# First layer of a two-layer graph network: SyncE's loads tied to steps of their own turn, half the buffers for a chunk's node rows, and a reordered turn

## The chip, the cores and the metric

The kernel runs on one core of a Trainium2 chip. The time of a run is that of the device, from the start of the program to its end, in microseconds (us). Lower is better. The kernel before was run three times; beside these there is one execution taken by the hardware profiler, and all durations below are from that one.

The engines that matter are PE (TensorE, matrix products), DVE (VectorE), ACT (ScalarE), POOL (GpSimd, which does nothing in this kernel's loops but issue indirect DMAs that gather rows) and SP (SyncE, which issues all other DMAs). Each engine works through its own list of instructions in order. A wait on a semaphore holds up everything behind it on that engine.

## What is computed

There are 12,500 nodes with 128 features, and 400,000 edges sorted by the node at which they end (`dst`). Two layers follow one another; the change concerns the first, an edge and node perceptron, with a sum over the edges of each node:

```python
h = jnp.maximum(_layernorm(x, axis=-1), 0.0)
# _L0_gnn_ref
src_f = node_features[src]
dst_f = node_features[dst]
edge_in = jnp.concatenate([src_f, dst_f, edge_features], axis=1)
h = jax.nn.relu(edge_in @ We1 + be1)
edge_msg = jax.nn.relu(h @ We2 + be2)
node_in = jnp.concatenate([dst_f, edge_msg], axis=1)
h2 = jax.nn.relu(node_in @ Wn1 + bn1)
node_msg = jax.nn.relu(h2 @ Wn2 + bn2)
agg = jax.ops.segment_sum(node_msg, dst, num_segments=node_features.shape[0])
return node_features + agg
```

The second layer normalises the nodes again, multiplies each by eight matrices (one for each type of edge), gathers for every edge the row of its source and type, weighs it and sums by `dst`:

```python
H = jnp.einsum('ni,rio->rno', h, W)
msg = (H[etype, src] + b[etype]) * norm
out = jax.ops.segment_sum(msg, dst, num_segments=h.shape[0])
```

The eight products of a node are made in the first layer already, as soon as its sum is complete, and written to a table in HBM (`tab_h`).

## The kernel before

**Stages.** Up to about 130 us the nodes are normalised and multiplied, and two tables are written: `tab_a`, a row of 32 numbers per node for its part as a source in the first product, and `tab_cb`, a row of 96 for its part as an end in the first and third products. Then the first layer runs up to about 5433 us, and the second from there to the end. The second layer is bound by its own gathers on POOL (line 1019) and is the same in both kernels.

**Tiles.** Edges are taken in chunks of 1024 (8 tiles of 128), 391 in all. Three chunks make a span (131 spans). The edges of a span end in a window of nodes; a window's sums stand in one PSUM tile, `acc`, while the span's chunks are added to it. A window's end rows are read from `tab_cb` as a [126, 96] tile of bfloat16, 23.6 KB per chunk, `win`.

**The work of a chunk** is a class, `Edges`, whose methods are steps:

- `load_win` (L402): SP loads `win`, from a ring of 8 buffers.
- `ends_T` (L406): DVE compares the chunk's ends with the window's rows and writes a 0/1 matrix `ohT`.
- `gather_a` (L387): POOL issues eight indirect DMAs, each for 128 sources' rows of `tab_a`, into `gb`, a ring of 16. POOL can so run up to 16 chunks ahead of the rest.
- `first` (L420, L422): PE multiplies the edge features by their weights into the PSUM bank `pre` and adds the ends' part, `win` times `ohT`.
- `first_src` (L427, L431): DVE transposes `gb` to `agT`, which frees the gather's buffer, and adds it to `pre`, giving `z`. `first_end` (L435): ACT makes `h1` from `z`.
- `second` (L442, L447): PE products into banks `pm0` and `pm1`, and ACT to `em`.
- `third` (L453, L456, L459): PE products `win` x `ohT` and `em` x weights into bank `u`, and ACT to `h2`. This is the last step that reads `win`.
- `fourth` (L466): PE products into `pq0` and `pq1`. `fourth_sum` (L474, L475): DVE adds the bias, ACT takes the positive part rounded to PE's short form. `fourth_end` (L480): DVE takes what the rounding left out.
- `ends` (L485): DVE writes a 0/1 matrix `oh`. `fifth` (L494): PE adds the chunk to `acc`.

**The work of a span.** `head(s)` (L588) loads a span's five addresses from SBUF to SP's registers. `load_relb` (L595) brings 756 KB, repeated over partitions, which `ends_T` reads. `load_eat` (L602) brings 768 KB of edge features, which `first` reads. Both have two buffers. `Span(s)` (L687) loads the 128 nodes of the window, 64 KB, `xt`; `deviate` and `begin` normalise them. When the span's `acc` is complete, `end` sums it, and `rows_h` (L546 to L567) goes on as a generator, a piece at each `node_step()`: deviation, normalisation, a PE transpose into a bank (L558), ACT to `hT`, two PE products of 512 columns (L565), and SP's write of the rows to `tab_h` (L567), 576 KB.

**PSUM** has eight banks with one buffer for each name: `pre`, `pm0`, `pm1`, `u`, `pq0`, `pq1`, `acc`, and one with constants. A step that writes a bank waits for those who read it last.

**The loop** (L746 to L779) runs in turns. In turn i the chunk i is gathered and has its first product; chunk i-1 has its second and third, chunk i-2 its fourth and its values, and chunk i-3 is added up. With `s, k = divmod(i, 3)`, a turn has k = 0, 1 or 2. After the loop a written-out tail finishes the last chunks. At its end one call fixes the order on SP, DVE, ACT and PE to that of the program:

```python
in_order(start, ENG.SP, ENG.DVE, ENG.Activation, ENG.PE)
```

So the order of calls in a turn is the order on each queue. POOL's own order is that of the program too. `next(prepared)` hands out small pieces of a preparation for the second layer, one per turn in the earlier part of the loop.

Of the kernel before, what the change touches and what calls it, by code (L numbers as in the profile page):

```python
# [8 lines left out]
F32 = mybir.dt.float32  # L9
F32R = mybir.dt.float32r  # L10
BF16 = mybir.dt.bfloat16
# [9 lines left out]
P = 128  # L21
# [32 lines left out]
def gnn_kernel(  # L54
# [337 lines left out]
    class Edges:  # L392
# [5 lines left out]
            self.pool, self.psum, self.iota, self.node = pool, psum, iota, node  # L398

        def load_win(self, row):  # L400
            self.win = self.pool.tile([WR, 96], BF16, name="win", bufs=8)
            nc.sync.dma_start(in_bytes(self.win), row)  # L402

        def ends_T(self, relb):
# [165 lines left out]
    with tc.tile_pool(name="e0", bufs=2) as pool, \  # L570
# [5 lines left out]
        nc.vector.tensor_copy(nid_p, nid)  # L576
        chunks, spans, rows, relbs, eats = {}, {}, {}, {}, {}
        active = []
        before = [None]

        def node_step():
# [3 lines left out]
        def head(s):  # L585

            if s < NS:
                _, rows[s] = nc.values_load_multi_w_load_instructions(  # L588
                    heads[0:1, s, :], engines=[ENG.SP], min_val=0, max_val=RX * ROW * (N - 1),
                    skip_runtime_bounds_check_because="a least dst is a node")  # L590
# [89 lines left out]
        class Span:  # L680


            def __init__(self, s):
                _, _, _, at_x, at_h = rows.pop(s)
                self.to = from_byte(tab_h, at_h, P, N - 1)
                self.xt = pool.tile([P, D], F32, name="xt")
                nc.sync.dma_start(in_bytes(self.xt), from_byte(x, at_x, P, N - 1))  # L687

            def deviate(self):
# [5 lines left out]
            def end(self, left):  # L695

                before[0] = summed(pool, self.acc, "a20")
                banks = ("u", "u", "u") if left else ("pre", "pm0", "pm1")
                steps = rows_h(pool, psum, self.to, self.x0, before[0], banks)
                active.append(steps)  # L700
                if left:
                    node_step()
                else:
                    next(steps)
                    next(steps)
# [25 lines left out]
        def end_T(c):  # L731
            chunks[c].ends_T(relbs[c // SC][:, c % SC, :])
# [1 line left out]
        def first(c):  # L734
            chunks[c].first(eats[c // SC][:, c % SC, :])

        head(0)
        load_relb(0)
        load_eat(0)
        for c in range(AHEAD):  # L740
            load(c)
        end_T(0)


        L = NC - 1
        for i in range(L):  # L746
            s, k = divmod(i, SC)
            if k == 0:
                head(s + 1)
                load_relb(s + 1)  # L750
            load(i + AHEAD)
            if k == 1:
                load_eat(s + 1)
                spans[s] = Span(s)
            gb = gathered(i)
            first(i)
            if i > 0:
                chunks[i - 1].second()
            whole = sum_up(i - 3) if i > 2 else None
            chunks[i].first_src(gb)  # L760
            if i > 1:
                chunks[i - 2].fourth()
            if i > 0:
                chunks[i - 1].third()
            chunks[i].first_end()
            end_T(i + 1)
            if i > 1:
                ends(i - 2)
            if i % SC == 0:
                node_step()  # L770
            if i > 1:
                valued(i - 2)
            if i % SC == 0 and i:
                spans[i // SC - 1].deviate()
            node_step()
            if whole:
                whole.end(NC - (i - 2))
            if i % SC == 1 and i > 1:
                spans[i // SC - 1].begin()  # L779
            next(prepared, None)  # L780


# [4 lines left out]
                if L - c:  # L787
                    spans[c // SC + 1].begin()

        for s in range((L - 1) // SC, NS):  # L790
            if s not in spans:
                spans[s] = Span(s)
            spans[s].deviate()
        spans[(L - 1) // SC].begin()
        gb = gathered(L)
        first(L)
# [313 lines left out]
```

## Time and profile before

| | us |
|---|---|
| median of 3 runs | 9815.11 (9800.64 to 9815.46) |
| profiled execution | 9814.24 |
| its span in the profile | 9812.5 |
| PE busy | 3925.3 (40%) |
| DVE busy | 5313.4 (54%) |
| ACT busy | 1657.7 (17%) |
| POOL busy | 6275.8 (64%) |
| first layer's gathers on POOL, last start | 5265.75 |
| second layer's first gather | 5433.08 |

The profiled execution lies within 1 us of the median. A busy share is an average over both layers; the two have different limits. For the first layer, the following view gives each engine's busy time in two stretches, one while POOL still gathers and one after its last gather (length, busy us of PE, PEld, DVE, ACT and POOL, each with its number of instructions, PE's granted clock, the DMA engines' share, GB/s):

```profile
5100.00:5200.00 100.00, 61.50 (x230) 28.77 (x226) 55.03 (x99) 26.74 (x51) 58.15 (x62) 0.79 0.27 80
5300.00:5340.00 40.00, 35.59 (x151) 16.05 (x150) 34.95 (x61) 17.04 (x31) 0.00 (x0) 1.00 0.17 58
```

In the first stretch no engine is busy for more than 62% of the time; in the second PE and DVE are busy for close to 90%.

In a row of the costliest groups, the figures are busy time and mean duration (ns), then the idle time of that engine just before these instructions, and what ended most of it. "<-remote" means that a semaphore ended the wait that the profile can't put down to an instruction of this core's engines. In timelines, brackets hold the same for one instruction.

### The profile page before, as it was taken

How to read it: one execution, taken by the hardware profiler on the slowest of the kernel's cores; microseconds unless marked ns; L12 is line 12 of the kernel's file. 1: busy time of each engine (PE TensorE's matmuls, PEld its weight loads, DVE VectorE, ACT ScalarE, POOL GpSimd, SP SyncE). 2: the span in 40 equal slices, each digit the busy share in tenths (PEclk: the TensorE clock that was granted, in tenths of full speed). 3: DMA queues.
4: the chain of work that ended last, by engine and by line, in shares of the span. 5: the costliest groups of instructions: out<-in, count | busy, mean ns of one | idle time of the engine just before them, and what ended most of it. 6: DMA issues, size and time to landing. Idle time of an engine off the chain costs nothing.

```text
span 9812.5 us, 56126 instructions
## 1 busy us (share of the span) xinstructions
PE 3925.3 (40%) x13981; PEld 1895.2 (19%) x13982; DVE 5313.4 (54%) x8291; ACT 1657.7 (17%) x3217; POOL 6275.8 (64%) x6273
## 2 busy tenths in 40 slices
PE   2566666666666666666667100000000000000000
PEld 1233333333333333333233000000000000000000
DVE  4455555555555555555557555555555555555554
ACT  2222222222222222222223000000000000000000
POOL 6555555555555555555552677777777777777776
PEclk6777777777777777777778555555555555555555
DMA  3233332222222222222222111111111111111111
GB/s 120 74 87 66 72 72 72 70 65 68 66 66 66 71 71 66 67 66 69 64 72 77 56 51 51 51 51 51 51 51 51 51 51 51 51 51 51 51 51 46
DMA packets 605555, 614.49 MB, mean 63 GB/s; under 512 B 361633, under 2 KB 465893, under 8 KB 604767
## 3 DMA queue, kind: packets, MB, share of 16 engines
q1 hardware_dynamic: 403064, 353.77, 11.8%
q0 software_dynamic: 200192, 256.65, 10.4%
q8 instruction: 114, 1.87, 0.1%
q14 instruction: 221, 1.80, 0.1%
q10 hardware_dynamic: 1964, 0.41, 0.0%
HBM read 509.91 MB, written 100.43 MB: 62 GB/s over the span
## 4 chain that ended last, share of the span: by engine, by line
POOL 32%; PE 20%; another core or an unknown queue 17%; issue 17%; DVE 8%; ACT 4%; DMA 2%; DVEq 0%; POOLq 0%; SPq 0%; ACTq 0%
POOL hg L1019 31%; PE pq L466 5%; PE acc L494 3%; PE pm L442 3%; PE pre L420 3%; DVE nm L480 2%; ACT em L447 2%; PE u L456 1%; ACT h L459 1%; DMA hg<-tab_h,hidx_sb 1%; PE u L565 1%; PE pre L422 1%; ACT h L435 1%; DVE ohT L406 1%
## 5 line engine op out<-in xcount | busy, mean ns | idle before, releaser
L387 POOL DMA_INDIRECT gb<-tab_a,src_sb x3032 | 2862.1, 944 | 2211.8 <-DVE agT L427 1348.6
L1019 POOL DMA_INDIRECT hg<-tab_h,hidx_sb x3128 | 3282.0, 1049 | 1237.7 <-issue 994.2
L1026 DVE TENSOR_TENSOR v<-hg,io_p 128x1024 f32<-128x1024 f32 x782 | 960.0, 1228 | 2068.2 <-DMA hg<-tab_h,hidx_sb 2055.9
L994 PE MATMUL acc<-hm,oh 128*128 128x256 f32 x782 | 347.7, 512 | 3963.6 <-DVE oh L989 3435.6
L474 DVE TENSOR_TENSOR pq<-pq,b_n 128x512 f32<-128x512 f32 x782 | 530.5, 696 | 1443.6 <-remote 1089.3
L994 PEld LDWEIGHTS acc<-hm,oh 128*128 128x128 f32 x782 | 205.8, 304 | 4124.3 <-issue 4088.9
L1030 DVE TENSOR_REDUCE sm<-v 128x128 f32<-128x1024 f32 x782 | 959.0, 1226 | 9.1
L466 PE MATMUL pq<-w_n,h 128*128 128x256 f32 x3128 | 876.4, 431 | 0.0
L480 DVE SCALAR_TENSOR_TENSOR nm<-pq,nm 128x512 fp32r<-128x512 f32 x782 | 503.9, 686 | 666.4 <-ACT nm L475 369.3
L1033 ACT CAST hm<-sm 128x256 fp32r<-128x256 f32 x391 | 145.5, 372 | 4225.2 <-DVE sm L1030 2764.2
L459 ACT ACTIVATE h<-u,b_n 128x512 f32<-128x512 f32 x391 | 268.7, 687 | 2715.9 <-remote 1713.0
L466 PEld LDWEIGHTS pq<-w_n,h 128*128 128x128 f32 x3128 | 667.6, 224 | 97.6 <-issue 1.5
L494 PE MATMUL acc<-nm,oh 128*128 128x256 f32 x3128 | 615.5, 343 | 4.1 <-DVE nm L480 2.8
L442 PE MATMUL pm<-h,w_e 32*128 32x512 f32 x1564 | 556.4, 794 | 103.1 <-ACT h L435 59.8
L447 ACT ACTIVATE em<-pm,b_e 128x512 f32<-128x512 f32 x782 | 493.1, 681 | 554.8 <-PE pm L442 414.5
L494 PEld LDWEIGHTS acc<-nm,oh 128*128 128x128 f32 x3128 | 496.6, 230 | 421.7 <-issue 153.0
L420 PE MATMUL pre<-eats,w_ea 128*64 128x512 f32 x782 | 538.4, 778 | 93.8 <-DMA win<-tab_cb 92.7
L558 PE MATMUL u<-ident,t 128*128 128x128 f32 x130 | 57.3, 441 | 1208.9 <-ACT h L459 1176.6
L565 PE MATMUL u<-w_f,hT 128*128 128x512 f32 x520 | 317.1, 694 | 453.1 <-ACT h L459 384.9
L406 DVE TENSOR_TENSOR ohT<-relb,io_p 126x1024 bf16<-126x1024 bf16 x391 | 477.8, 1222 | 18.4 <-DMA relb<-rel_d 6.4
L485 DVE TENSOR_TENSOR oh<-io_p,rel_s 128x1024 fp32r<-128x1024 f32 x391 | 476.1, 1218 | 0.0
L456 PE MATMUL u<-em,w_msg 128*64 128x512 f32 x1564 | 414.7, 598 | 31.7 <-ACT em L447 20.0
(122 smaller groups left out, 3773.5 us busy)
## 6 DMA issues: line engine op xcount, KB each, us to landing
eats<-in_ea SPq DMA_DIRECT2D x131, 768.0 KB
relb<-rel_d SPq DMA_DIRECT2D x131, 756.0 KB
tab_h<-ht SPq DMA_DIRECT2D x131, 576.0 KB
hg<-tab_h,hidx_sb POOLq DMA_INDIRECT x3128
gb<-tab_a,src_sb POOLq DMA_INDIRECT x3032
win<-tab_cb SPq DMA_DIRECT2D x391, 23.6 KB
xt<-in_x SPq DMA_DIRECT2D x131, 64.0 KB
xw<-tab_h SPq DMA_DIRECT2D x131, 64.0 KB
```

Source lines behind the costliest of these rows:

```text
L387: nc.gpsimd.indirect_dma_start(out=gb[:, t, :], out_offset=None, in_=tab_a, in_offset=bass.IndirectOffsetOnAxis(ap=idx(t), axis=0))
L406: nc.vector.tensor_tensor(self.ohT, relb, self.node.to_broadcast([WR, CE]), op=OP.is_equal)
L420: nc.tensor.matmul(self.pre, w_ea, eat, start=True, stop=False)
L442: nc.tensor.matmul(pm, w_e2[rows, :], self.h1[rows, :], start=True, stop=True)
L447: nc.scalar.activation(em, pms[h], AF.Relu, bias=b_e2)
L466: nc.tensor.matmul(pq[:, 2 * i:2 * i + 2, :], self.h2[:, P * (2 * k + i):P * (2 * k + i) + P], w_n2, start=True, stop=True)
L480: nc.vector.scalar_tensor_tensor(nm[:, :, 1, :], pq, 0.0, nm[:, :, 0, :], op0=OP.max, op1=OP.subtract)
L494: nc.tensor.matmul(acc, self.oh[:, i, :], self.nm[:, at, :, :].rearrange("p q d -> p (q d)"), start=(start and i == 0), stop=(stop and i = ...
L994: nc.tensor.matmul(acc[:, 0:2 * D], oh[:, q, :], hm[:, q, :, :].rearrange("p r d -> p (r d)"), start=begin and q == 0, stop=stop and q == 1)
L1019: nc.gpsimd.indirect_dma_start(out=hg[:, t - c * CT, :], out_offset=None, in_=tab_hr, in_offset=bass.IndirectOffsetOnAxis(ap=hidx_sb[:, t: ...
L1026: nc.vector.tensor_tensor(v, hg, w_p[:, q, t:t + CT, None].to_broadcast([P, CT, D]), op=OP.mult)
L1030: nc.vector.tensor_reduce(sm[:, q, :], v.rearrange("p t d -> p d t"), AX.X, OP.add)
```

## The change

All edits are in the first layer's loop and its helpers:

- `win` has a ring of 4 buffers, not 8. Three chunks are loaded ahead in both kernels, so chunk i+3's load takes the buffer of chunk i-1.
- `load(i + 3)` moves from the head of turn i to behind the turn's `third(i - 1)`.
- `head` and `load_relb` are for span s+2, in the turn k = 1, behind `end_T(i + 1)`; before, they were for span s+1, at the head of the turn k = 0. `load_eat` is for span s+2, in the turn k = 2, behind `first(i)`; before, for span s+1 in the turn k = 1. The two spans that come first are loaded ahead of the loop.
- `xt` has one buffer, not the pool's two. `Span(s)` is made in the turn k = 0, behind `begin` of the span before; the last span has a buffer of its own name. `deviate` moves to the turn k = 1.
- The order of the other steps in a turn changes: `first_end` comes ahead of `fourth`, `ends` and `end_T` behind it; the addition of the fourth product's bias comes ahead of `third`, and `fourth_end` behind it.
- The node's transpose and its two products go to bank `pre` while the loop runs, and to `u` in the tail, as they did throughout before.

No transfer and no arithmetic is added or left out.

```diff
-            self.win = self.pool.tile([WR, 96], BF16, name="win", bufs=8)
+            self.win = self.pool.tile([WR, 96], BF16, name="win", bufs=4)
...
+        node_banks = ["pre"] * 3
...
-                self.xt = pool.tile([P, D], F32, name="xt")
+                self.xt = pool.tile([P, D], F32, name="xt" if s < NS - 1 else "xt_last", bufs=1)
...
-                banks = ("u", "u", "u") if left else ("pre", "pm0", "pm1")
+                banks = node_banks if left else ("pre", "pm0", "pm1")
...
-        head(0)
-        load_relb(0)
-        load_eat(0)
-        for c in range(AHEAD):
-            load(c)
+        for s in range(2):
+            head(s)
+            load_relb(s)
+            load_eat(s)
+            if s == 0:
+                for c in range(AHEAD):
+                    load(c)
         end_T(0)
...
             s, k = divmod(i, SC)
-            if k == 0:
-                head(s + 1)
-                load_relb(s + 1)
-            load(i + AHEAD)
-            if k == 1:
-                load_eat(s + 1)
-                spans[s] = Span(s)
             gb = gathered(i)
             first(i)
+            if k == SC - 1:
+                load_eat(s + 2)
             if i > 0:
                 chunks[i - 1].second()
             whole = sum_up(i - 3) if i > 2 else None
             chunks[i].first_src(gb)
+            chunks[i].first_end()
             if i > 1:
                 chunks[i - 2].fourth()
+                ends(i - 2)
+            end_T(i + 1)
+            if k == 1:
+                head(s + 2)
+                load_relb(s + 2)
+            if k == 0:
+                node_step()
+            if i > 1:
+                chunks[i - 2].fourth_sum()
+            node_step()
             if i > 0:
                 chunks[i - 1].third()
-            chunks[i].first_end()
-            end_T(i + 1)
             if i > 1:
-                ends(i - 2)
-            if i % SC == 0:
-                node_step()
-            if i > 1:
-                valued(i - 2)
-            if i % SC == 0 and i:
-                spans[i // SC - 1].deviate()
-            node_step()
+                chunks[i - 2].fourth_end()
+            load(i + AHEAD)
+            if k == 0:
+                if s:
+                    spans[s - 1].begin()
+                spans[s] = Span(s)
+            if k == 1:
+                spans[s].deviate()
+            if i == L - 2:
+                for s in range(s + 1, NS):
+                    spans[s] = Span(s)
+            if i == L - 1:
+                for s in range(s + 1, NS):
+                    spans[s].deviate()
             if whole:
                 whole.end(NC - (i - 2))
-            if i % SC == 1 and i > 1:
-                spans[i // SC - 1].begin()
             next(prepared, None)
...
+        node_banks[:] = ["u"] * 3
         spans[(L - 1) // SC].begin()
```

More of the change, by code (lines that the diff above doesn't have):

```diff
@@ L788, in ended @@
                     spans[c // SC + 1].begin()
[L790 to L793, printed above, removed]
+        node_banks[:] = ["u"] * 3
         spans[(L - 1) // SC].begin()
```

## The prediction

> **What bounds the kernel now.** I read the costliest groups first, then the end-of-chain shares, then one span (three chunks, three turns) turn by turn. Turn boundaries are the starts of the transpose of gathered rows (VectorE, L427). Layer 0 ends near 5433 us; layer 1 (to 9812 us) is not touched.
>
> ```profile
> POOL 32%; PE 20%; another core or an unknown queue 17%; issue 17%; DVE 8%; ACT 4%; DMA 2%; DVEq 0%; POOLq 0%; SPq 0%; ACTq 0%
> ...
> L387 POOL DMA_INDIRECT gb<-tab_a,src_sb x3032 | 2862.1, 944 | 2211.8 <-DVE agT L427 1348.6
> ...
> L459 ACT ACTIVATE h<-u,b_n 128x512 f32<-128x512 f32 x391 | 268.7, 687 | 2715.9 <-remote 1713.0
> ...
> L558 PE MATMUL u<-ident,t 128*128 128x128 f32 x130 | 57.3, 441 | 1208.9 <-ACT h L459 1176.6
> ```
>
> There is one core, so "another core or an unknown queue" (17%) can't be another core: something holds engines up that the profile can't name. ACT waits 1713.0 us for a "remote" releaser before L459, in layer 0 alone, and PE's node transpose then waits 1176.6 us for L459. POOL, which only gathers, still loses 1348.6 us to L427, which frees its buffers. Windows of a span (length; busy PE, PEld, DVE, ACT, POOL; PE clock, DMA share, GB/s):
>
> ```profile
> 2494.90:2506.75 11.85, 11.03 (x39) 5.45 (x40) 7.63 (x14) 4.10 (x9) 7.55 (x8) 0.81 0.07 12
> 2506.75:2516.19 9.44, 8.62 (x41) 4.26 (x40) 7.83 (x15) 3.40 (x7) 6.61 (x7) 1.00 0.13 35
> 2516.19:2533.84 17.65, 6.20 (x24) 2.48 (x22) 7.12 (x13) 3.69 (x8) 8.50 (x9) 0.70 0.39 126
> ```
>
> The third (k=0) turn takes 17.65 us although no engine works more in it. The timeline inside it, idle time and releaser in brackets:
>
> ```profile
> 2517.47 0.37 SPq L595 DMA_DIRECT2D relb<-rel_d  x1
> 2518.40 1.03 PE L456 MATMUL u<-em,w_msg 128*64 128x512 f32 x4
> 2518.70 2.83 SPq L402 DMA_DIRECT2D win<-tab_cb  x2
> 2522.95 1.38 SPq L602 DMA_DIRECT2D eats<-in_ea  x1
> 2525.03 0.70 SPq L687 DMA_DIRECT2D xt<-in_x  x1
> 2526.19 0.95 POOL L387 DMA_INDIRECT gb<-tab_a,src_sb  x1 [0.30 <-issue]
> 2527.13 0.01 SPq L402 DMA_DIRECT2D win<-tab_cb  x1
> 2527.88 0.70 DVE L474 TENSOR_TENSOR pq<-pq,b_n 128x512 f32<-128x512 f32 x1 [7.46 <-remote]
> 2530.14 0.69 ACT L459 ACTIVATE h<-u,b_n 128x512 f32<-128x512 f32 x1 [12.66 <-remote]
> 2530.88 0.48 PE L558 MATMUL u<-ident,t 128*128 128x128 f32 x1 [11.46 <-ACT h L459]
> 2534.56 0.94 POOL L387 DMA_INDIRECT gb<-tab_a,src_sb  x1 [7.42 <-DVE agT L427]
> ```
>
> PE's product for L459 is done at 2519.43 (2518.40 + 1.03), yet ACT starts at 2530.14. Just then SP, released by the table write L567 at 2514.82, issues the whole next span's loads in one burst, while POOL gathers. DVE and ACT go on when the burst and POOL's last free buffer end together (2527.13, 2526.19 + 0.95). A control lies in the same trace. After POOL's last gather (5265.75) SP issues the same six loads at usual pace:
>
> ```profile
> 5292.14 0.37 SPq L595 DMA_DIRECT2D relb<-rel_d  x1
> 5292.67 0.84 SPq L402 DMA_DIRECT2D win<-tab_cb  x2
> 5293.61 0.41 SPq L602 DMA_DIRECT2D eats<-in_ea  x1
> 5294.12 0.42 SPq L687 DMA_DIRECT2D xt<-in_x  x1
> 5294.64 0.36 SPq L402 DMA_DIRECT2D win<-tab_cb  x1
> ```
>
> From the first of these to the last is 2.5 us, not 9.7 (2517.47 to 2527.13); no engine stands, and the next three transposes (5290.92, 5298.39, 5306.69, 5316.12) span 25.2 us, not 39.9. So I read the standing as an effect of SP's burst and POOL's gathers together; each alone (k=1 and 2 turns; the tail) shows none. What in the burst does it, its length or any single issue, the trace doesn't tell.
>
> **What the Trainium skill says.** "SBUF — State Buffer", Who interferes with whom: DMA has its own ports and doesn't contend with engines. The trace disagrees in effect: 12.66 us of ACT standing on a finished product, only where two issuers are active; it must lie in issuing or signalling, not in ports. "DMA: Bandwidth & Descriptors", Issuing engines are not separate DMA queues: transfers of SyncE and GpSimd interleave on the same 16 engines. That fits two issuers hindering one another, though the DMA share in the slow turn is only 0.39. "Perfetto Trace Analysis", Optimization Strategy: a gap that repeats on the engine to be saturated can mean too few buffers; POOL's 7.42 us fits, but as the consequence, since the consumer stands. "TensorE: Matmul & The Clock Gate", Part 1: The HAM clock gate: PE slows after idling; it agrees, the clock is 0.70 and 0.81 around the gap and 1.00 in the k=2 turn.
>
> **The change part by part.**
>
> *Loads spread, each behind a wait.* Same loads, same bytes. With 4 win buffers, chunk i+3's load takes chunk i-1's buffer, last read by third(i-1) of this turn; so SP parks every turn. relb waits for end_T, eats for first, xt (one buffer) for begin. SP issues two, two or three and two transfers in the turns k=0, 1, 2 (the table write among them), not seven at once. Queued behind a waiting load on SP are only further loads, the table write and the preparation's copies. Lead is two turns for win, near 20 us, four turns for relb and eats, one for xt (its readers come in the k=1 turn); 768 KB arrives beside gathers at 126 GB/s in 6 us, so late transfers cost nothing. If that cover were gone, PE's first product would wait; "pre <- win" is 92.7 us now.
> Gain: POOL's idle time per span is 7.42 us in the k=0 turn and 3.15 and 2.16 us in others (gaps before POOL's first gather after each transpose), the total 1348.6. Gone, the next limit is POOL itself: 8 x (0.944 + 0.30 idle between, 1.248 measured from start to start) = 9.99 us per chunk. DVE's 7.6 to 7.8 us and PE's (25.2 / 3 = 8.4 us in the tail at full clock) lie beside it.
> Sum: the 49th of 3128 gathers starts at 133.3 us, and 3080 x 1.2485 on top gives 3979; about 55 us of early idle stay (an estimate: the first two spans take 81.5 and 102.8 us, as tables and preparation come in): last gather at 4034. Before, POOL was 16 chunks ahead and layer 1 began 167 us after the last gather; a bound POOL has no lead, so only the last chunk's way through remains: 30 us from the last transpose (5403.0) to 5433.1, plus landing and two chunks in flight, say 50. Layer 1 begins at 4084 instead of 5433: -1349. Against the profiled 9814.24 (span 9812.5 + 1.7 around) that is 8465. I add 75 for turns that exceed 9.99 us (0.57 us per span of 131), since node steps make one turn in three heavier: 8540. The median 9815.11 is within 1 us of the profiled run, so no shift.
>
> *The turn reordered.* third moves after fourth, ends, end_T and the sums; h1 goes ahead of h2 on ACT, so second(i) has its input sooner; h2 is used one turn later (fourth), as before. fourth_sum's ACT part (2 x 0.5 us) now precedes h2. No work is added; hidden by 1.5 us or more of slack per turn on each engine under POOL's 9.99. Without this cover it is at worst one ACT round, 0.7 + 1.1 us per turn x 391 = 700 us; at best -0.5 us per turn where PE bounds (-200). I take nothing.
>
> *Node product in "pre".* It no longer waits for L459's read of "u": 1176.6 + 384.9 us stand at those waits, nearly all stall. Instead "pre" must be read by z (DVE) first and the next first() waits for hT and ht's reads. With the stall gone it is hidden; alone it is worth at most 0.8 us x 2 per span = 200 us, at worst +200.
>
> *head ahead by a span, three heads' registers live.* SP only, 2.2 us each, as before.
>
> **Rivals.**
> A, as above, own range 8400 to 8800: 0.58.
> B, the stall is only partly cured. For: SP still issues two or three transfers per turn while POOL gathers. If half of the 10.5 us per span POOL gaps stays, 5.3 x 131 = 690 come back: 9230 (8800 to 9790): 0.14.
> C, no change: another cause of standing, e.g. gathers with any transfer, or PE at half clock as bound (12 us a turn: 2533.84 to 2546.68 shows 12.84), 3 x 13 = 39 us a span, today's: 0.04. Against it: the k=2 turn at 9.44 us and clock 1.00.
> D, slower: a single released issue suffices, and once it has begun the standing lasts until POOL runs out of free buffers. For: today it ended as POOL stopped (2527.14). Then what SP paid once per span it pays in several turns. If in the two turns with big transfers, POOL's idle is 2 x 7.4 + 3.1 = 17.9 us per span against 10.6 (7.4 + 3.1): +7.3 x 130 = +950: 10,760. If in all three, 22.2: +11.6 x 130 = +1510: 11,320. It decides from the point at which more than 10.6 us of POOL idle per span arises. Against it: the table write at 2514.82 is itself one released issue during gathers, and no engine stood at once; the start-up (133 to 150 us) has SP and POOL busy together without it: 0.24.
>
> **How the numbers follow.** A and B are faster, 0.72; C 0.04; D 0.24. What can be told from no change is about 0.2%, 20 us; C's band. The time is A's, 8540. Low 8400 is under the sum of 8465 by the 55 us early idle; the range reaches through B, C and the milder half of D (10,800), leaving out about 0.12 of D and 0.05 of A.
>
> **What would show it.** Right: L387's idle before, by L427, from 1348.6 to under 200; remote at L459 from 1713.0 to under 200; k=0 turns near 10 us; layer 1's first gather near 4100; SP's transfers one or two per turn at 0.4 us; L558 with output "pre". B: remote waits of several us in the turns with relb or eats. D: L427's share above 2000 and several slow turns per span. Wrong in another way: L420 waiting for win or eats (late loads), or L427 waiting for landed gathers.

## The result, and the profile after

The changed kernel takes 9700.92 us (median of 4 runs, 9688.48 to 9707.97) against 9815.28 us of the kernel before (4 runs, three of them those of the table ahead): a ratio of 0.988, 95% interval 0.9862 to 0.9898. The forecast was 8540. The profiled execution took 9694.5 us, its span is 9692.6.

In some of the experiments both kernels take about 7950 us, and the standing that the forecast speaks of isn't there; so each run below stands beside the kernel before as it was measured with it. "A chip with the standing" means below that the kernel before took about 9800 us there; what tells such a chip from another is left open.

The changed kernel (chain by engine, then groups: busy, mean ns, idle before and what ended it):

```profile
POOL 32%; DVE 19%; issue 16%; another core or an unknown queue 15%; PE 14%; DMA 3%; DVEq 0%; ACT 0%; POOLq 0%; SPq 0%; ACTq 0%
...
L387 POOL DMA_INDIRECT gb<-tab_a,src_sb x3032 | 2868.2, 946 | 2088.3 <-DVE agT L427 1235.1
...
L474 DVE TENSOR_TENSOR pq<-pq,b_n 128x512 f32<-128x512 f32 x782 | 524.8, 696 | 1891.0 <-remote 1413.4
...
L459 ACT ACTIVATE h<-u,b_n 128x512 f32<-128x512 f32 x391 | 268.7, 687 | 177.5 <-PE u L456 90.8 <-issue 40.8 <-remote 36.8
...
L420 PE MATMUL pre<-eats,w_ea 128*64 128x512 f32 x782 | 533.2, 771 | 1504.3 <-DVE ht L566 1325.5
```

The unknown releaser is still there, 15% of the chain instead of 17%. Before, it stood ahead of ACT's L459 (1713.0 us) and of DVE's L474 (1089.3); now L459 has 36.8 us of it and L474 has 1413.4. PE's wait has moved from the node transpose (L558, 1208.9 us before) to the first product L420, which shares the bank `pre` with the node's products. POOL's wait for L427 fell from 1348.6 to 1235.1 us: these 113.5 us are most of the 119.9 by which the second layer starts earlier. The second layer itself takes 4379.4 us in both traces (from its first gather, at 5433.08 and 5313.16, to the span's end).

The windows of one span, from transpose to transpose, the turns k = 0, 1 and 2 (length; busy PE, PEld, DVE, ACT, POOL; PE clock, DMA share, GB/s):

```profile
2487.64:2495.35 7.71, 5.91 (x31) 3.22 (x29) 7.25 (x14) 3.90 (x8) 5.47 (x6) 1.00 0.11 16
2495.35:2514.61 19.26, 7.71 (x30) 3.56 (x30) 7.10 (x12) 3.74 (x7) 9.65 (x11) 0.77 0.20 56
2514.61:2527.49 12.88, 12.88 (x41) 6.35 (x40) 8.02 (x15) 4.05 (x8) 7.56 (x8) 0.68 0.36 119
```

The turn k = 0 has shrunk from 17.65 to 7.71 us, the long turn is now k = 1 with 19.26, and the three together take 39.85, as long as a span did before. The timeline inside it:

```profile
2498.36 0.95 POOL L387 DMA_INDIRECT gb<-tab_a,src_sb  x1 [0.31 <-issue]
...
2499.09 1.02 PE L565 MATMUL pre<-w_f,hT 128*128 128x512 f32 x2
2499.16 0.35 SPq L596 DMA_DIRECT2D relb<-rel_d  x1
...
2507.11 0.94 POOL L387 DMA_INDIRECT gb<-tab_a,src_sb  x1 [0.30 <-issue]
2510.92 1.30 DVE L474 TENSOR_TENSOR pq<-pq,b_n 128x512 f32<-128x512 f32 x2 [11.79 <-remote]
...
2511.71 1.14 ACT L475 ACTIVATE nm<-pq 128x512 fp32r<-128x512 f32 x2 [13.37 <-DVE pq L474]
...
2512.86 1.97 PE L420 MATMUL pre<-eats,w_ea 128*64 128x512 f32 x2 [11.55 <-DVE ht L566]
...
2515.32 0.94 POOL L387 DMA_INDIRECT gb<-tab_a,src_sb  x1 [7.27 <-DVE agT L427]
```

SP issues one transfer here and then waits; there is no burst. Yet DVE stands 11.79 us on a product that PE has made by the trace's account (PE has gone on to L453 and L456), and goes on when POOL has stopped. The profile models the ends of PE's instructions, so whether the product is late or only the signal of it, no run here tells. The burst was spread as the change says, and the standing came all the same, once per span, in another turn.

To count standings, take PE's semaphore in the trace: the time from the end of a PE instruction that raises it to the next recorded rise. The trace lacks many rises (in the kernel before it has 2793 for 4125 instructions that raise it), so of such a stretch only the longest part counts in which neither DVE nor ACT starts on a product of PE. Over 5 us, between 600 and 5000 us, the kernel before has 108 standings (1096 us in all), the changed one also 108 (1299 us). In 102 of the latter, POOL issues seven more gathers within the standing. In the spans around 2500 us they begin 10.0 us into an uninterrupted POOL run of 19.7 us (two chunks), and end 2.1 to 2.8 us after the run.

### The profile page after: what moved, and what is told of

Its sections match the earlier page's. It is cut to its first block, busy times and chain, and to the rows that moved or that the text cites. A ratio compares the mean times of both kernels' runs of the same rounds, so it can differ in the third digit from the quotient of the medians.

```text
span 9692.6 us, 56697 instructions
## 1 busy us (share of the span) xinstructions
PE 3870.6 (40%) x13981; PEld 1935.7 (20%) x13982; DVE 5295.4 (55%) x8291; ACT 1737.3 (18%) x3217; POOL 6288.0 (65%) x6273
## 4 chain that ended last, share of the span: by engine, by line
POOL 32%; DVE 19%; issue 16%; another core or an unknown queue 15%; PE 14%; DMA 3%; DVEq 0%; ACT 0%; POOLq 0%; SPq 0%; ACTq 0%
POOL hg L1028 30%; DVE pq L474 4%; PE pq L466 3%; PE acc L494 3%; PE pre L420 3%; PE pm L442 3%; DVE oh L485 3%; DVE nm L480 3%; DVE ohT L406 2%; DVE z L431 2%; POOL gb L387 2%; DVE ht L566 1%; DMA hg<-tab_h,hidx_sb 1%; DVE agT L427 1%
## 5 line engine op out<-in xcount | busy, mean ns | idle before, releaser
L387 POOL DMA_INDIRECT gb<-tab_a,src_sb x3032 | 2868.2, 946 | 2088.3 <-DVE agT L427 1235.1
L474 DVE TENSOR_TENSOR pq<-pq,b_n 128x512 f32<-128x512 f32 x782 | 524.8, 696 | 1891.0 <-remote 1413.4
L420 PE MATMUL pre<-eats,w_ea 128*64 128x512 f32 x782 | 533.2, 771 | 1504.3 <-DVE ht L566 1325.5
L475 ACT ACTIVATE nm<-pq 128x512 fp32r<-128x512 f32 x782 | 454.4, 598 | 2425.6 <-DVE pq L474 1977.5
L494 PE MATMUL acc<-nm,oh 128*128 128x256 f32 x3128 | 639.5, 350 | 63.0 <-DVE nm L480 43.3
L420 PEld LDWEIGHTS pre<-eats,w_ea 128*64 128x64 f32 x782 | 99.0, 159 | 1808.4 <-DVE ht L566 1459.2
L456 PE MATMUL u<-em,w_msg 128*64 128x512 f32 x1564 | 418.3, 604 | 35.7 <-ACT em L447 20.2
L431 DVE TENSOR_TENSOR z<-pre,agT 64x256 f32<-64x256 f32 x782 | 325.8, 417 | 147.9 <-PE pre L422 47.4
```

What stands on the lines that cost most here:

```text
L387: nc.gpsimd.indirect_dma_start(out=gb[:, t, :], out_offset=None, in_=tab_a, in_offset=bass.IndirectOffsetOnAxis(ap=idx(t), axis=0))
L420: nc.tensor.matmul(self.pre, w_ea, eat, start=True, stop=False)
L474: nc.vector.tensor_add(pq, pq, b_n2[:, None, :].to_broadcast([P, 4, D]))
L494: nc.tensor.matmul(acc, self.oh[:, i, :], self.nm[:, at, :, :].rearrange("p q d -> p (q d)"), start=(start and i == 0), stop=(stop and i = ...
```

## The experiments

**First: what of SP's work begins it.** In the changed kernel the standings begin within 1 us of relb's issue, and the register loads of `head` stand just ahead.

e1, relb for two spans only; e3, padded rows; e4, other rows:

```diff
 # e1
-            if s < NS:
+            if 1 < s < NS:
+                relbs[s] = relbs[s % 2]
+            elif s < NS:
                 relbs[s] = pool.tile([WR, SC, CE], BF16, name="relb", bufs=2)
 # e3
-                relbs[s] = pool.tile([WR, SC, CE], BF16, name="relb", bufs=2)
+                relbs[s] = pool.tile([WR, SC, CE + 16], BF16, name="relb", bufs=2)[:, :, 0:CE]
 # e4
-                rel_d[s * SC:s * SC + SC, :].rearrange("(o c) e -> o c e", o=1)
-                .to_broadcast([WR, SC, CE])
+                rel_d[0:WR * SC, :].rearrange("(p c) e -> p c e", c=SC)
```

e2 moves `head(s + 2)` from ahead of `load_relb(s + 2)` to behind `Span(s)`.

> The changed kernel with relb loaded for the first two spans only; later spans compare their ends with those old rows, so the sums differ, while every other transfer and all arithmetic stay in number and size. In the changed kernel PE's results stop reaching DVE for 11 to 13 us once per span, within 1 us of relb's transfer being issued, five register loads just ahead of it. Theory R (relb's transfer begins the standing): it is gone, POOL's wait for L427 falls from 1235 us to under 250, time 8450 to 8700. Theory H (the register loads of head begin it): the standing stays, time within 1% of 9700. Theory T (the place in the turn begins it, whatever SP does there): within 1% of 9700.

> The changed kernel with the five register loads of head(s + 2) moved from ahead of relb's load (turn k = 1) to the end of the turn k = 0, behind the load of xt. Theory R: one long standing per span still begins within 1 us of relb's issue; time 9600 to 9800. Theory H: it begins with the register loads at the end of the turn k = 0, away from relb. Theory T: as R in place, but then e1 keeps it too.

> The changed kernel with relb's rows padded in SBUF by 32 bytes, so that its transfer of 756 KB is cut into 378 packets of 2048 bytes, as that of eats (384 of 2048), and not 126 of 6144; the same HBM rows are still read by all 126 partitions. If the long packets begin the standing (theory R, size): gone, 8450 to 8700. If one row read by all partitions does (theory R, same row): stays, 9600 to 9800. Theory H: stays.

> The changed kernel with relb's transfer reading another 6144 bytes of rel_d for each partition, instead of the same for all: 126 packets of 6144 bytes as before, but from 126 places in HBM, so that the ends compared are others and the sums differ. If one row read by all partitions begins the standing: gone, 8450 to 8700. If the long packets do: stays, 9600 to 9800. Theory H: stays.

Measured: 7945.4, 7943.17, 7943.64 and 7948.17 us, and the kernel before on this chip 7957.12. None has a standing over 3 us in the first layer, so they tell no theory from another. They tell something else. The groups of POOL in e2, whose work is the changed kernel's:

```profile
L1028 POOL DMA_INDIRECT hg<-tab_h,hidx_sb x3128 | 2951.3, 944 | 992.6 <-issue 936.9
L387 POOL DMA_INDIRECT gb<-tab_a,src_sb x3032 | 2864.7, 945 | 924.1 <-issue 812.3
```

POOL no longer waits for L427; nearly all its idle time is the 0.30 us between gathers. The first layer's last gather starts at 3979.81 us and the second layer's first at 4020.3. The second layer's gathers take 1.248 us from start to start in the mean, against 1.392 in the traces before and after. Where the standing is absent, the changed kernel is thus bound by POOL. The kernel before took only 14 us more there (7957.12), so POOL probably bounds it too; no trace of it was taken on such a chip.

e5, the kernel of e1 again:

> The kernel of e1_relb_twice once more: relb loaded for the first two spans only, so that the sums differ. The kernel before took 7957 us beside e1 to e4, against 9815 us beside the changed kernel, so that chip doesn't show the standing at all and e1 to e4 could not tell its beginning. If the kernel before takes about 9815 us beside this run: theory R 8450 to 8700 and POOL's wait for L427 under 250 us; theories H and T within 1% of 9700. If it takes about 7957 us: 7945, as in e1, and the question stays open.

Measured: 9695.43 us, the kernel before 9799.19. Its timeline, without any transfer of relb:

```profile
2500.68 0.36 SPq L690 DMA_DIRECT2D xt<-in_x  x1
...
2504.48 1.02 PE L565 MATMUL pre<-w_f,hT 128*128 128x512 f32 x2
...
2512.46 0.94 POOL L387 DMA_INDIRECT gb<-tab_a,src_sb  x1 [0.30 <-issue]
2514.87 0.70 DVE L474 TENSOR_TENSOR pq<-pq,b_n 128x512 f32<-128x512 f32 x1 [10.36 <-remote]
...
2520.11 0.94 POOL L387 DMA_INDIRECT gb<-tab_a,src_sb  x1 [6.71 <-DVE agT L427]
```

The standing has its old place and nearly its old length. Theory R falls.

e6 (heads in the turn k = 2, behind eats) and e7 (one register load per span) were to part H from T:

```diff
 # e6
             if k == SC - 1:
                 load_eat(s + 2)
+                head(s + 2)
...
             if k == 1:
-                head(s + 2)
                 load_relb(s + 2)
 # e7
...
+                at = 0 if s < 2 else SC + 1
...
-                    heads[0:1, s, :], engines=[ENG.SP],
+                    heads[0:1, s, at:], engines=[ENG.SP],
...
+                if s < 2:
+                    rows0.append(got)
+                rows[s] = list(rows0[s % 2][0:at]) + list(got)
```

> The changed kernel with the five register loads of head(s + 2) moved from the turn k = 1 to the turn k = 2, behind the load of eats, which waits for this turn's first product; the register loads are thus some 12 to 19 us later in the span. In e5 relb's transfer was gone and the standing kept its place and length, so theory R has fallen. On a chip on which the kernel before takes about 9815 us: theory H (SP's register loads beside POOL's gathers begin the standing, which lasts until POOL pauses): the long standing leaves the turn k = 1 and begins within 3 us of the register loads in the turn k = 2. Theory T (something of PE's, DVE's or ACT's own work in the turn k = 1 begins it): it stays in the turn k = 1, just behind the node products L565. On a chip without the standing: about 7945 us, and the question stays open.

> The changed kernel with one register load per span instead of five: the table's address is loaded, the four others are those of the first two spans for good, so win and xt hold rows of the first spans and the sums differ. On a chip on which the kernel before takes about 9815 us: theory H with each register load holding signals up by itself: the standing falls from 12 us to a fifth or less, time below 8900. Theory H with the first load enough: standing stays, 9600 to 9800. Theory T: standing stays, 9600 to 9800. On a chip without the standing: about 7945 us.

Measured: 7943.11 and 7945.34 us, the kernel before 7953.1: the question stayed open there. But the traces at hand weaken H: of the kernel before's 108 standings, 18 begin 9 us or more after the last register load, and one of them, from 678.20 to 689.04 us, lies between two issues of SP at 658.69 and 694.35. The run e15 below, with the register loads in another turn, decides it.

**Second: POOL's gathers.** e8 halves them; e9 keeps their number but lets POOL wait for the turn (`half` gathers four tiles of the chunk 14 ahead, `pause` lets GpSimd copy one element of the tile named).

```diff
 # e8
-        gb = gpool.tile([P, CT, 32], F32, name="gb", bufs=16)
-        for t in range(CT):
+        gb = gpool.tile([P, CT // 2, 32], F32, name="gb", bufs=16)
+        for t in range(CT // 2):
...
-            nc.vector.transpose(agT, gb.rearrange("p t f -> p (t f)"))
+            for half in range(2):
+                nc.vector.transpose(agT[:, 128 * half:128 * half + 128],
+                                    gb.rearrange("p t f -> p (t f)"))
 # e9
-            gb = gathered(i)
+            half(i + LEAD, 0)
+            gb = gbs.pop(i)
             first(i)
...
             chunks[i].first_end()
+            if i + LEAD < NC:
+                pause(chunks[i].h1)
+            half(i + LEAD, 1)
...
                 chunks[i - 1].third()
+                if i + LEAD < NC:
+                    pause(chunks[i - 1].h2)
```

> The changed kernel with four gathers per chunk instead of eight: the transpose is made twice from the four gathered tiles, so the second half of the source rows is wrong and the sums differ; DVE has one small instruction more per turn, all else stays. Theory G (formed on the traces: PE's results are held up whenever POOL has gathered without a pause for some 10 us, until it pauses, whatever SP does): POOL now gathers 5 us per turn and must pause, so the long standings are gone; the first layer falls to some 27 us a span as after the last gather (25.2), time 7900 to 8300 where the kernel before takes about 9800. Theory T (the work of the turn k = 1 begins it) or H (SP's register loads begin it, POOL's gathers only prolong it): standings of 5 us or more once per span stay, 30 to 36 us a span, 8500 to 9300. Where the kernel before takes about 7955: 7250 to 7600, as POOL bounds there, and nothing is told apart.

> The changed kernel with the gathers of a chunk in two halves, issued 14 chunks ahead, and POOL waiting after each half: for this turn's h1 after the first, for h2 of the chunk before after the second (it copies one element of each). So POOL can't gather more than 4 to 8 times while PE's results are held up. Theory G: no standing is longer than about 8 us (4 more gathers, 5 us, and 2.8 us), against 12.5; how many there are is open, time 9000 to 9700. Theory H or T with a standing that has a length of its own: 12 us standings once per span stay, and POOL's pauses come on top, 9800 to 10400. Where the kernel before takes about 7955: 7950 to 8300.

Measured: e8 7216.1 and e9 8104.77 us, the kernel before 7948.35: again a chip without the standing. Three repeats (e10, e13 and e14) met such chips too (e10, the kernel of e8: 7205.81; e13 and e14, that of e9: 8123.79 and 8109.56; the kernel before 7950.57 to 7967.3). e8 gives a measure: with POOL out of the way the second layer begins at 3293 us, 727 us earlier than in e2. The next two met a chip with the standing.

> The kernel before, unchanged, to have its profile beside e12. Where it takes about 7955 us: no standing of 5 us or more in the first layer, POOL gathering without a pause at 1.25 us a gather, so that the same program, with its burst of loads on SP, does without the standing. Where it takes about 9800: as in the profile shown.

> The kernel of e8_half_gathers (four gathers per chunk, used twice). Where the kernel before takes about 9800 us: theory G 7900 to 8300, no standing of 5 us or more; theory T or H 8500 to 9300, with standings of 5 us or more once per span. Where it takes about 7955: 7210, as in e8 and e10.

Measured: e11 9862.94 us (POOL's wait for L427 1384.4 us, much as in the profile before) and e12 7689.63, the kernel before 9800.99. The first and the last of these are the same kernel, so single runs can lie 62 us apart, and differences of that size between single runs say nothing here. e12's chain and POOL's group:

```profile
POOL 40%; DVE 31%; issue 19%; PE 8%; DMA 1%; ACT 0%; DVEq 0%; another core or an unknown queue 0%; SPq 0%; POOLq 0%; ACTq 0%
...
L387 POOL DMA_INDIRECT gb<-tab_a,src_sb x1516 | 1433.1, 945 | 1574.4 <-DVE agT L428 1223.9
```

The unknown releaser is gone from the chain, and between 600 and 3130 us no standing is longer than 2.7 us (e8 has none over 1 us), although SP's loads, the register loads and PE's, DVE's and ACT's work are those of the changed kernel, but for one small transpose per turn. The second layer begins at 3301.43 us, within 9 us of e8 on the other chip. POOL's wait is now harmless: it is done early and waits for the consumer. Theories H and T, which kept long standings, did not hold here (7.9 us a turn, 23.7 a span). Theory G's picture did, but its time, 7900 to 8300, was too high. The start of this trace says more: while POOL fills its 16 buffers, in one run of 76 gathers up to 167.1 us, DVE stands 16.2 us and ACT 14.6 on an unknown releaser; from then on POOL makes four gathers and pauses, and neither waits over 3 us for such a releaser again. The 2011.7 us by which the second layer begins earlier than in the changed kernel hold both the lost standings and POOL's lost work.

**Third: the parts of the change.** e15 puts SP's loads back as before (the later places, the second span loaded ahead and the single buffer of xt go too), and keeps order and bank. e17 (its file differs in one line) keeps loads and order, and puts the node's products back in `u`.

```diff
 # e15
-            self.win = self.pool.tile([WR, 96], BF16, name="win", bufs=4)
+            self.win = self.pool.tile([WR, 96], BF16, name="win", bufs=8)
...
             s, k = divmod(i, SC)
+            if k == 0:
+                head(s + 1)
+                load_relb(s + 1)
+            load(i + AHEAD)
+            if k == 1:
+                load_eat(s + 1)
+                spans[s] = Span(s)
             gb = gathered(i)
 # e17
-        node_banks = ["pre"] * 3
+        node_banks = ["u"] * 3
```

> The changed kernel with all of SP's loads back where the kernel before has them (8 buffers for win, two for xt, relb and head one span ahead at the head of the turn k = 0, eats and xt in the turn k = 1), so that SP issues them in one burst again; the new order of the turn and the bank of the node's product stay. Where the kernel before takes about 9800 us: if the loads' new waits brought the 114 us, 9780 to 9830; if the order and the bank did and the burst is without effect (theory G), 9680 to 9720. Where it takes about 7955: 7940 to 7955, and nothing is told apart.

Measured: 9674.75 us (4 runs), the kernel before 9813.02 (7 runs); ratio 0.9859, interval 0.9836 to 0.9882. SP's burst is back, and this is where it lies:

```profile
2483.11 0.37 SPq L596 DMA_DIRECT2D relb<-rel_d  x1
2483.64 0.84 SPq L402 DMA_DIRECT2D win<-tab_cb  x2
2483.80 0.95 POOL L387 DMA_INDIRECT gb<-tab_a,src_sb  x1 [3.36 <-DVE agT L427]
2484.58 0.41 SPq L603 DMA_DIRECT2D eats<-in_ea  x1
...
2485.09 0.42 SPq L688 DMA_DIRECT2D xt<-in_x  x1
2485.61 0.36 SPq L402 DMA_DIRECT2D win<-tab_cb  x1
...
2494.53 1.02 PE L565 MATMUL pre<-w_f,hT 128*128 128x512 f32 x2
...
2502.56 0.94 POOL L387 DMA_INDIRECT gb<-tab_a,src_sb  x1 [0.30 <-issue]
2503.60 0.70 DVE L474 TENSOR_TENSOR pq<-pq,b_n 128x512 f32<-128x512 f32 x1 [9.02 <-remote]
```

The same loads take 2.5 us, not 9.7, while POOL gathers. The standing begins at 2493.8, 8 us after the burst, when SP has nothing to do, and ends just after POOL's run. That is the rule: 108 of e15's 112 standings begin more than 4.5 us after the last register load, half of them 12.9 us or more, so theory H falls as well. The burst doesn't begin the standing and isn't slow by itself. From relb's issue to the sixth issue it takes 2.5 us (median) in the 102 of e15's 112 bursts that touch no standing, and 8.7 in the 10 that do; in the kernel before 93 of 110 touch one (9.65 us), and the 17 others take 3.65. So the burst was stretched by the standing.

The turn in which a standing falls goes with the order of the turn and the bank. It is k = 1 for 105 of 108 in the changed kernel and for 100 of 112 in e15, although their loads differ; k = 0 for 91 of 108 in the kernel before.

> The changed kernel with the node's transpose and its two products in the bank u again, as before; loads and order stay. e15 has shown that the 114 us don't come from the loads. Where the kernel before takes about 9800: if the bank brought them, 9780 to 9830; if the order did, 9680 to 9720. Where it takes about 7955: 7940 to 7960, and nothing is told apart.

Measured: 9833.27 us (13 runs), the kernel before 9813.25 (16 runs); ratio 1.0021, interval 1.0009 to 1.0034. Loads and order without the bank are worth nothing, a loss of 0.2% if anything. As e17 differs from the changed kernel in the bank alone, its ratio of 1.0021 beside 0.988 is what the bank is worth in the new order: 1.4%, some 135 us. PE's third product in e17 and then in e15:

```profile
L453 PE MATMUL u<-ohT,win 126*64 126x512 bf16 x782 | 200.3, 491 | 1830.0 <-DVE ht L566 1048.0 <-ACT hT L560 581.4 <-issue 112.5
```

```profile
L453 PE MATMUL u<-ohT,win 126*64 126x512 bf16 x782 | 160.5, 407 | 0.0
```

In the new order `third` follows the node steps, so with the node's products in `u` it waits for their readers, 1830.0 us in all. In `pre` that wait is gone, and a part of it comes back at L420. The bank alone in the old order was not tried.

e17's standings are fewer and shorter, 93 with 732 us in all, and spread over the turns k = 0, 1 and 2 (43, 21 and 29), and yet it is the slower kernel: the sum of standings isn't the time. And 62 of them lie beside POOL runs of one chunk, as this one, in a run of eight gathers from 2531.72 us:

```profile
2540.45 0.94 POOL L387 DMA_INDIRECT gb<-tab_a,src_sb  x1 [0.30 <-issue]
2543.56 1.30 DVE L474 TENSOR_TENSOR pq<-pq,b_n 128x512 f32<-128x512 f32 x2 [6.01 <-remote]
```

**Fourth: runs or number.** e12 halved the number of gathers and the length of POOL's runs together. e16 is the kernel of e9. e18 gives POOL other work after each chunk:

```diff
+        idle = gpool.tile([P, 7, D], F32, name="idle", bufs=1)
+        nc.gpsimd.tensor_tensor(idle, iota_f[:, None, :].to_broadcast([P, 7, D]),
+                                ident[:, None, :].to_broadcast([P, 7, D]), op=OP.subtract)
         return gb
```

> The kernel of e9_gathers_wait (gathers in two halves, POOL waiting for h1 and for h2), beside e17. Where the kernel before takes about 9800: theory G (a standing lasts until POOL pauses) no standing over about 8 us against 12.5, time 9000 to 9700; if the number of gathers decides and not the pauses, standings of 12 us stay, 9800 to 10400. Where it takes about 7955: 8105 to 8125, as in e9, e13 and e14.

Measured: 9691.83 us, the kernel before 9813.25. Standings of 11 to 12 us stayed (111 over 5 us), against theory G's 8, although the time lies in its range of 9000 to 9700; the other theory's, 9800 to 10400, was not met. POOL at the end of one, which lasts from 2457.39 to 2468.53:

```profile
2466.34 0.95 POOL L391 DMA_INDIRECT gb<-tab_a,src_sb  x1 [0.30 <-issue]
2471.99 0.18 POOL L766 COPY tick<-h 1x1 f32<-1x1 f32 x1 [4.71 <-ACT h L462]
```

POOL was behind: the results that it was to wait for had been made, and it issued eight gathers within the standing. It then stopped at the new wait for h2 and not for a buffer, and DVE went on 1.2 us later. So the wait came too late to shorten anything.

> The changed kernel with POOL subtracting two constant tiles (128 x 896, 1.68 us in the profile's first stage) after each chunk's eight gathers, into a tile that nobody reads: the number of gathers stays, but POOL never gathers longer than 10 us without a pause of about 2.1 us. In e16 the waits came too late to bite: POOL was behind and still made 8 gathers in each standing. In all traces with standings of 12 us these begin 10.0 us into a POOL run of 20 us and end with it. Where the kernel before takes about 9800: theory G (the length of POOL's uninterrupted runs) no standing over 5 us but few; POOL bounds at 8 x 1.248 + 2.0 = 12.0 us a turn, 36 us a span against 39.3, time 9150 to 9400. If the number of gathers decides and not the pauses: standings of 10 us or more stay and POOL's pauses come on top, 9700 to 10400. Where it takes about 7955: 8600 to 8800, and nothing is told apart.

Measured: 10302.23 us, the kernel before 9821.58. That is in the range of the second forecast, but the pauses did not lie where they were meant to, so it counts for neither. POOL's order is not among those that `in_order` fixes; it need not be the program's, as is said ahead of the prediction. All 391 subtractions began before 1678 us, four to ten between two chunks:

```profile
940.82 0.96 POOL L387 DMA_INDIRECT gb<-tab_a,src_sb  x1
...
949.58 0.95 POOL L387 DMA_INDIRECT gb<-tab_a,src_sb  x1 [0.30 <-issue]
950.54 8.56 POOL L391 TENSOR_TENSOR idle<-iota_f,ident 128x896 f32<-128x896 f32 x4
952.14 0.45 DVE L430 STREAM_TRANSPOSE agT<-gb 128x256 f32<-128x256 f32 x1 [11.00 <-DMA gb<-tab_a,src_sb]
```

In that stretch (600 to 1600 us) POOL gathers 10 us and then subtracts for 8 us or more. It has lost its lead, and DVE waits for the gathers to land (L430). The 13 turns in which PE's semaphore doesn't rise for over 5 us all hold such a wait, so they are no standings, and neither DVE nor ACT waits over 3 us for an unknown releaser. At 1680 us the subtractions end, and POOL gathers without a pause up to 1870.3 to win back its lead. At once DVE and ACT stand again, up to 46.47 us:

```profile
1797.77 0.95 POOL L387 DMA_INDIRECT gb<-tab_a,src_sb  x1 [0.31 <-issue]
1798.17 0.70 DVE L477 TENSOR_TENSOR pq<-pq,b_n 128x512 f32<-128x512 f32 x1 [46.47 <-remote]
1799.02 0.95 POOL L387 DMA_INDIRECT gb<-tab_a,src_sb  x1 [0.30 <-issue]
```

So in one trace, by one program, the standing is absent while POOL gathers with long pauses and present when it gathers without. It can end while POOL gathers on, and by e17 a run of one chunk with short pauses is enough for a short one. The first part of e18 has runs of eight gathers as well, so the length of a run alone doesn't decide. Whether the pauses do, or the gathers per time, no run parts; both differ in e12 and e18. What in the gathers does it stays open.

## Why the prediction was wrong

**The failed step** is the reading that carried the rest: "So I read the standing as an effect of SP's burst and POOL's gathers together", and with it the loads' spreading as a gain of 1349 us. Two observations were behind it. The burst and the standing lay at the same time; e15 shows that the burst is quick by itself and that the standing comes 8 us later without it. And the tail showed the burst without a standing; but there POOL had stopped, and e12 shows that with half the gathers the standing goes whatever SP does. The turns k = 1 and k = 2 were no control for SP, as POOL's and PE's state differed there too.

The trace before held a better control, its start. The prediction puts the first two spans' 81.5 and 102.8 us down to tables and preparation; but SP issues nothing from 150.95 to 295.21 us, POOL gathers without a pause up to 272.8, and ACT and DVE stand all the same:

```profile
150.60 0.35 SPq L402 DMA_DIRECT2D win<-tab_cb  x1
...
218.72 0.69 ACT L459 ACTIVATE h<-u,b_n 128x512 f32<-128x512 f32 x1 [38.51 <-remote]
...
271.83 0.94 POOL L387 DMA_INDIRECT gb<-tab_a,src_sb  x1 [0.30 <-issue]
...
274.72 0.70 DVE L474 TENSOR_TENSOR pq<-pq,b_n 128x512 f32<-128x512 f32 x1 [40.87 <-remote]
...
295.21 2.26 SPq L634 DMA_DIRECT2D dst_d<-tr  x4
```

In e2, without the standing, the same two spans take 20.6 and 25.0 us.

The loads' new waits bring nothing: 0.9859 without them, 0.988 with them, with intervals that overlap.

**What took its place.** Once a span the standing returned, in the turn k = 1. Three of the signs named for a right forecast came: the unknown wait at L459 fell to 36.8 us, the turn k = 0 to 7.71, and SP issues one or two transfers a turn. The one that counts, L427's wait, did not fall: it is 1235.1 us and not under 200. Rival B's range, 8800 to 9790, covers the result, and its sign, a wait in the turn with relb, came too, but by luck: the wait stays when relb isn't loaded (e5), and the standing wasn't halved, it was 1096 us before and 1299 after, and only moved. Rival D's remark that a standing lasts until POOL runs out of free buffers fits most of the changed kernel's (2.1 to 2.8 us after the last gather in the spans around 2500 us), although no single issue of SP starts it, and although e18's of 46.47 us ended while POOL gathered on. Rival C's first half, another cause and gathers among it, was nearest, at 0.04.

**The node's bank** I took as nothing, "at most" 200 us. In the new order it is the whole of the gain: with it the changed kernel is 114 us faster than the kernel before, without it (e17) 20 us slower, a difference of some 135 us. The term was inside its bound and the value taken was wrong; I had priced the wait that the bank takes from the node's product, and not the one that `third` gets in the new order if the bank stays.

**The order of the turn** at nothing: loads and order together are +0.2% (e17), inside the bound of 700.

**The sum for a first layer bound by POOL** was right where the standing is absent. It said 3979 us for the last gather without early idle, 4034 with it, and 50 us on to the second layer. e2 has 3979.81 and 40.5. The 55 us of early idle, worked out from the first two spans, did not come, as those spans' length was the standing. But there the kernel before is probably bound by POOL as well, and the change is worth some 14 us of 7957 (single runs).

## What to carry to other kernels

Two things that happen together in a trace, a burst of issues and a standing, may be stretched by a third; put the suspected cause back alone (or take it alone out) before pricing its removal. A stretch of a trace is a control only if it differs in the suspect alone: the tail differed in POOL's gathers as well as in what I looked at. Look also for the stretch in which the suspect is silent and the effect stays; here it was the start of the loop, in the trace that I already had. And when steps of a turn are reordered, ask for each PSUM bank who now stands between its last reader and its next writer: that was worth more here than all the moved loads.

## What the hardware showed

The same program takes 9800 us in some measurements and 7950 in others: the kernel before, measured eleven times beside the eighteen runs, took 9799 to 9822 us in five and 7948 to 7967 in six. The chips are numbered on record, 4, 6, 13 and 15 for the long times and 1, 2, 4 and 7 for the short ones. As number 4 is on both sides, it isn't shown that the chip itself makes the difference.

Where it takes 9800, DVE and ACT go on some 10 to 13 us after PE's product by the trace, about once a span, while POOL gathers, and up to 46.47 us while POOL gathers without a pause (e18); in e2 POOL gathers without one for 3900 us, and neither ever waits over 3 us for an unknown releaser. The second layer's gathers take 1.392 us in the mean instead of 1.248. The mean hides that about six in ten of them keep to 1.3 us in the kernel before, and that 1039 of the 1198 longer steps, up to 2.2 us, come after the fifth to eighth gather of an eight. The transfers themselves are not slower: a packet of 4096 bytes of these gathers takes 219 to 250 ns in the mean in the traces before, after, e11 and e12 and 221 to 251 in e2, e8 and e9. With half the gathers the first layer is the same on both (3301 and 3293 us to the second layer).

The sentence of the Trainium skill that the forecast cites ("SBUF — State Buffer", Who interferes with whom: DMA doesn't contend with an engine) is about ports of the memory. The forecast read the standing against it. No run here shows that a port is what PE's products wait for, so the traces neither bear the sentence out nor contradict it. An unknown releaser in the chain can depend on where or when the program runs, as it does here, and not on the program alone.
